# Reordering a chunk's last slot, the norm statistics and the first six front steps in a two-layer convolution kernel

## The chip, the cores and the metric

The kernel runs on one core of a Trainium2 chip. The metric is device time in microseconds: the median of several runs of the whole program, 5571.28 us for the kernel before (three runs, 5568.5 to 5586.93 us). One further execution was taken by the hardware profiler; every view below comes from it.

## The reference

Eight images of 256 channels and 64x64 pixels, float32, go through two layers with a residual each:

```
# layer 0, on gn(x): a group norm over 32 groups of channels
qkv = w_qkv . gn(x)                            # 1x1, 256 -> 768
attn = softmax(q . k over the 3x3 neighbours)  # 4 heads
out  = beta * (attn . v's 3x3 patches) + alpha * (generated 3x3 kernel . v's patches)
x1   = x + w_proj . out
# layer 1, on gn(x1): deformable 3x3 convolution
om   = conv3x3(gn(x1), w_off) + b_off          # 18 offsets and 9 masks for each pixel
v    = bilinear sample of gn(x1) at 9 shifted places, times sigmoid(mask)
y    = x1 + sum over the 9 places of w[:, :, place] . v
```

## The kernel before

**Two streams of work are woven into one order.** The *front* of an image is layer 0 and the preparation of layer 1: the generators `attention` (L550) and `prepare` (L617), run by `fronts` (L745), which stops at each `yield`. What lies between two yields is a *step*; an image has STEPS = 73 of them (L54). The *back* of an image is the sampling and the big convolution. Its unit is a *slot*: one of 9 places of one of 8 chunks of 8 rows (512 pixels), so 72 slots for an image. The loop at L875 walks over the 576 slots of all images and puts front steps between them. The order on TensorE (PE), ScalarE (ACT), VectorE (DVE) and GpSimd (POOL) is the order in which the Python code issues (`manual_schedule`, L854); the DMA queue of SyncE (SP) is ordered by the framework. PE's order, ACT's and DVE's are thus three lists made by the same walk, and a wait on one of them holds up whatever was issued behind it on that engine.

**The back.** Four *blocks* of 128 pixels make a slot. For each block `gather` (L758, POOL) fetches four corners of every pixel, 512 KB, by an indirect DMA into one of 10 buffers `g`; `scale` (L772, ACT) writes the first weighted corner to a buffer `s`; `sum_corners` (L783, DVE) adds the other three for two blocks at once, six instructions at line L788. `ahead(i)` (L792) issues two scales 8 blocks ahead of block i, the sums of two blocks 6 ahead, and two gathers 18 ahead (14 ahead in the last image, by LAST_GATHERS). `transposes` (L808) turns a slot's four `s` on PE (L815, tile `pt`) and copies them to `v` (L818, ACT, tile `vt`). `product` (L821) multiplies one slot's `v` with the weights of its place and accumulates in `po` (L832, PE), one PSUM tile with one buffer for a whole chunk. After a chunk's ninth product `finished` (L840) adds `po` and the residual in two DVE instructions (L843, tile `r`) and sends the result out from SP (L844). The next chunk's first product writes the same `po`, and so waits for L843.

**Order within slot n** (L875 to L891): transposes of slot n; `ahead(4n)`; product of slot n-1; the front steps that are due (one, and at times two); if slot n-1 ended a chunk, `finished`; `ahead(4n+2)`. I call a slot n with n divisible by 9 an *edge*. On DVE an edge therefore reads: sums 4n+6 and 4n+7, the step's DVE work, the two L843, sums 4n+8 and 4n+9.

**Steps.** A norm starts with `Norm` (L192): `bn_aggr` over a chunk-wise statistic (L199, DVE), a tiny matmul (L201, PE, tile `gn`) and four small DVE instructions; `ready` (L209) in the next step has a second tiny matmul (L212), a square root on ACT and a reciprocal; `normed` (L218, L228, DVE) then writes normalised rows `xn`. Each attention chunk has seven steps, which I name by their PE work:
A: `spread_weights` of the chunk before (L475 on PE, evacuated at L483 by DVE, tile `wk`, four PSUM buffers) and `q` (L276);
B: `k` (L308, evacuated by ACT);
C: `products` (L346, evacuated at L354 by DVE) and the first half of `weighted` (L516);
D: `logits` (DVE), the second half of the value transposes, `generated`;
E: first half of `v` (L308, evacuated at L330 by ACT), second half of `weighted`, `turned` (L398 on PE, L402 on DVE), `normed`;
F: second half of `v`, half of `project` (L528, added by DVE at L539), `softmax_3` (DVE);
G: the other half of `project`, statistics (L543), `weights` (L462), the first half of the value transposes.
Then come a closing step that projects the last chunk, the second norm, and nine preparation steps: `positions` (from L665; DVE from L682), `to_table` (L629), `offsets` (L649), statistics of the next image (L258). All these share four PSUM buffers, `ps_a` (L185), in turn: a PE group that needs a fifth waits until the first has been evacuated.

**Ahead of the loop** the whole front of image 0 and STEPS_AHEAD = 6 steps of image 1 (its first norm, then A to D of its first chunk) are issued (L859). After that 73 steps are spread over each 72 slots, so a period of 72 slots is the back of one image beside the front of the next; the last period has no front beside it.

Of the kernel before, what the change touches and what calls it, by code (L numbers as in the profile page):

```python
# [9 lines left out]
F32 = mybir.dt.float32  # L10
# [7 lines left out]
P = 128  # L18
C = 256
NT = C // P  # L20
# [5 lines left out]
NB = N // P  # L26
NC = H // R
KK = 9
# [18 lines left out]
SLOTS = NC * KK  # L47
BLOCKS = SLOTS * NB
SUM_AHEAD = 6
SCALE_AHEAD = SUM_AHEAD + 2  # L50
GATHERS = 10
LEAD = SCALE_AHEAD + GATHERS
LAST_GATHERS = 6
STEPS = 2 + 7 * NC + 6 + NC + 1  # L54
STEPS_AHEAD = 6

# [2 lines left out]
def preact_kernel(ctx: ExitStack, tc: tile.TileContext, a: dict, out: bass.AP):  # L59
# [19 lines left out]
    B = x.shape[0]  # L79
# [64 lines left out]
    with (  # L144
# [26 lines left out]
        for i in range(min(2, B)):  # L171
# [3 lines left out]
            for o in range(H * WP, ENTRIES, P):  # L175
                n = min(P, ENTRIES - o)
# [4 lines left out]
    p1 = ctx.enter_context(tc.tile_pool(name="p1", bufs=1))  # L181
# [7 lines left out]
    def psum_a(name):  # L189
        return ps_a.tile([P, 512], F32, tag="a", name=name)  # L190

    class Norm:  # L192


        def __init__(self, stats, name):
            self.name = name
            mv = p1.tile([P, NT, 2], F32, tag="mv", name=f"mv_{name}")
            for ct in range(NT):
                nc.vector.bn_aggr(mv[:, ct, :], stats[:, ct].rearrange("p c s -> p (c s)"))  # L199
            ps = psum_a(f"gn_{name}")  # L200
            nc.tensor.matmul(ps[:, 0:NT], gmat, mv[:, :, 0], start=True, stop=True)  # L201
            self.gn = gn = p2.tile([P, 2, NT], F32, tag="gn", name=f"gn_{name}")
            nc.vector.tensor_copy(gn[:, 0, :], ps[:, 0:NT])
            self.d = d = p1.tile([P, NT], F32, tag="gnd", name=f"gnd_{name}")
            nc.vector.tensor_sub(d, mv[:, :, 0], gn[:, 0, :])
            nc.vector.tensor_mul(d, d, d)
            nc.vector.tensor_add(d, d, mv[:, :, 1])
# [10 lines left out]
    def normed(xt, gn, c):  # L218

        xn = xn2[c % 2]  # L220
        lo, hi = max(0, R * c - 1), min(H, R * c + R + 1)
        if c == 0:
            nc.vector.memset(xn[:, :, 0, :], 0.0)
        if c == NC - 1:
            nc.vector.memset(xn[:, :, R + 1, :], 0.0)
        o = lo - (R * c - 1)
        for ct in range(NT):
            nc.vector.tensor_scalar(  # L228
                xn[:, ct, o : o + hi - lo, 1 : W + 1],
                xt[:, ct, lo * W : hi * W].rearrange("p (r w) -> p r w", w=W),  # L230
                gn[:, 0, ct : ct + 1],
                gn[:, 1, ct : ct + 1],
                ALU.subtract,
                ALU.mult,
            )
        return xn
# [13 lines left out]
        return t[:, ct, dy : dy + R, dx : dx + W]  # L250

    stats0: dict = {}

    def first_stats(b, c):
        if c == 0:
            stats0[b] = p2.tile([P, NT, NC, 6], F32, tag="stats0", name=f"stats0_{b}")
        for ct in range(NT):
            nc.vector.bn_stats(  # L258
                stats0[b][:, ct, c, :], image[:, ct, c * N : (c + 1) * N]
            )  # L260

    class Attention:

# [286 lines left out]
    def attention(b):  # L550

        xt = image
        gn = Norm(stats0.pop(b), f"0_{b}")
        stats = p2.tile([P, NT, NC, 6], F32, tag="stats", name=f"stats1_{b}")
        yield None
        gn = gn.ready()
        xn = normed(xt, gn, 0)
        yield None
        d = None
        for c in range(NC):  # L560
            a_ = Attention(b, c, xn, stats)
            if d:
                d.spread_weights()
            a_.q(0)
            a_.q(1)
            yield None
            a_.k(0)
            a_.k(1)
            yield None
            a_.products()  # L570
            if d:
                d.weighted(0)
            yield None
            a_.logits()
            if d:
                d.keys(1)
                d.carry_v()
            a_.generated()
            a_.softmax_1()
            a_.carry_k()  # L580
            yield None
            a_.v(0)
            if d:
                d.weighted(1)
            a_.turned()
            a_.softmax_2()
            if c + 1 < NC:
                xn = normed(xt, gn, c + 1)
            yield None
            a_.v(1)  # L590
            if d:
                d.add(0, d.project(0))
            a_.softmax_3()
            yield None
            if d:
                d.add(1, d.project(1))
                d.second_stats()
            a_.weights()
            a_.keys(0)
            yield None  # L600
            d = a_
        d.spread_weights()
        yield None
        d.weighted(0)
        d.keys(1)
        yield None
        d.weighted(1)
        yield None
        for m in range(NT):
            d.add(m, d.project(m))  # L610
        d.second_stats()
        yield None
        gn = Norm(stats, f"1_{b}")
        yield None
        yield gn.ready()

    def prepare(b, gn):  # L617
# [121 lines left out]
        if b + 1 < B:  # L739
            first_stats(b + 1, NC - 1)  # L740
# [17 lines left out]
    def gather(i):  # L758
        if i >= B * BLOCKS:
            return  # L760
        b, n = divmod(i, BLOCKS)
        c, k, j = n // NB // KK, n // NB % KK, n % NB
        g = gp.tile([P, 4 * C], F32, tag="g", name=f"g_{i}")
        nc.gpsimd.indirect_dma_start(  # L764
            out=g,
            out_offset=None,
            in_=tables[b % 2],
            in_offset=bass.IndirectOffsetOnAxis(ap=found[b, c][0][:, j, k : k + 1], axis=1),
        )
        rows[i] = g  # L770
# [21 lines left out]
    def ahead(i):  # L792

        scale(i + SCALE_AHEAD)
        scale(i + SCALE_AHEAD + 1)
        sum_corners(i + SUM_AHEAD)
        first = (B - 1) * BLOCKS
        for n in (i + LEAD, i + LEAD + 1):
            if n < first:
                gather(n)  # L800

        for n in (i + LEAD, i + LEAD + 1):
            if n - GATHERS + LAST_GATHERS >= first:
                gather(n - GATHERS + LAST_GATHERS)

    state: dict = {}

# [13 lines left out]
    def product(b, n):  # L821
        c, k = divmod(n, KK)
        if k == KK // 2:
            r = p1.tile([P, NT, N], F32, tag="r", name=f"r_{b}_{c}")
            nc.sync.dma_start(r, kept[b % 2][:, :, c * N : (c + 1) * N])
            state["r"] = r
        if k == 0:
            state["po"] = ps_o.tile([P, NT, 512], F32, tag="o", name=f"po_{b}_{c}")
        po, v = state["po"], state.pop(("v", n))
        for m in range(NT):  # L830
            for ct in range(NT):
                nc.tensor.matmul(  # L832
                    po[:, m, :],
                    w_conv[:, ct, k, m * P : (m + 1) * P],
                    v[:, ct, :],
                    start=(k == 0 and ct == 0),
                    stop=(k == KK - 1 and ct == NT - 1),
                )

    def finished(b, c):  # L840
        po, r = state["po"], state["r"]
        for m in range(NT):
            nc.vector.tensor_add(r[:, m], po[:, m], r[:, m])  # L843
        nc.sync.dma_start(  # L844
            out[b].rearrange("(t p) l -> p t l", p=P)[:, :, c * N : (c + 1) * N], r
        )
# [7 lines left out]
    with tc.manual_schedule(engines=ordered):  # L854
        for c in range(NC):
            first_stats(0, c)
        steps = fronts()
        done = 0
        while done < STEPS + STEPS_AHEAD:  # L859
            next(steps, None)  # L860
            done += 1
        for i in range(GATHERS):
            gather(i)
        for i in range(0, SUM_AHEAD, 2):
            if i == 0:
                scale(0)
                scale(1)
            scale(i + 2)
            scale(i + 3)
            sum_corners(i)  # L870
            gather(i + GATHERS)
            gather(i + GATHERS + 1)
        gather(SUM_AHEAD + GATHERS)
        gather(SUM_AHEAD + GATHERS + 1)
        for n in range(B * SLOTS + 1):  # L875
            if n < B * SLOTS:
                transposes(*divmod(n, SLOTS))
                ahead(NB * n)
            last = None
            if n > 0:  # L880
                b, h = divmod(n - 1, SLOTS)
                product(b, h)
                if h % KK == KK - 1:
                    last = b, h // KK
            while (done - STEPS - STEPS_AHEAD) * SLOTS < (n + 1) * STEPS:
                next(steps, None)
                done += 1
            if last:
                finished(*last)
            if n < B * SLOTS:  # L890
                ahead(NB * n + 2)  # L891


# [76 lines left out]
```

## Time and profile before

| what | value |
|---|---|
| median of three runs | 5571.28 us |
| the profiled execution: its own time | 5194.36 us |
| its span, first to last instruction | 5192.6 us |
| mean granted TensorE clock in it | 0.963 |
| from the start to the first product (L832) | 379.1 us |
| seven periods with a front beside them, each | 611 to 636 us |
| the last period, without one | 413.8 us |
| PE busy in the second period (628.2 us) | 586.0 us |
| DVE busy in it | 521.5 us |
| ACT busy in it | 293.1 us |

The profiled execution was 377 us (7%) shorter than the median of the runs, and nothing in the profile says why. Sums of durations below are made against 5194.36 us.

How to read the views: the page's first part gives busy time by engine (PEld is PE's weight load, which overlaps PE). The view by stretches gives busy time, granted clock (PEclk) and DMA load between two times. The view of waits says which engine stood idle before an instruction and what ended the idle time. The timeline lists instructions of an engine in order, equal neighbours merged: start, length, engine, line, operation, tiles out<-in, shape, count, and in brackets the idle time before them and who ended it.

### The profile page before, as it was taken

The page shows a single profiled execution, that of the slowest core. Times are in us where ns is not written, and L with a number is a line of the kernel's source. Part 1 is how long each engine was busy: PE and PEld are TensorE (multiplying, and loading weights), DVE is VectorE, ACT ScalarE, POOL GpSimd, SP SyncE. Part 2 cuts the span into 40 slices and gives each one's busy share as a digit, 9 for nine tenths or more (in the row PEclk, how much of TensorE's full clock was granted, in tenths as well). Part 3 has the DMA queues.
Part 4 walks back from the last instruction along what each step waited for, and adds up shares of the span by engine and source line. Part 5 has one row for each costly group of instructions (what it writes and reads, how often), then busy time and mean ns, then how long its engine had stood idle before and what let it go on. Part 6 is the DMA issues. An engine that isn't in the chain of part 4 may idle for free. (4 is left out here: it accounts for less than half of the span.)

```text
span 5192.6 us, 79716 instructions
## 1 busy us (share of the span) xinstructions
PE 4750.7 (91%) x26592; PEld 2643.4 (51%) x26592; DVE 4182.7 (81%) x10071; ACT 2360.6 (45%) x5184; POOL 3151.1 (61%) x2310
## 2 busy tenths in 40 slices
PE   6979999999999999989999999899999999998888
PEld 4545554555545555455554555445554455544443
DVE  4558788888888888788888888878888888877887
ACT  2334444444444444444444444444444444444544
POOL 0027665666657666566665666746666566666776
PEclk9989999999999999999999999999999999999999
DMA  2058778877797777977779777888778877788998
GB/s 91 21 180 277 266 273 304 300 267 257 275 322 280 268 269 260 337 262 273 279 267 324 273 260 262 287 291 285 268 265 296 297 274 267 267 296 313 388 379 337
DMA packets 476840, 1422.60 MB, mean 274 GB/s; under 512 B 46910, under 2 KB 114750, under 8 KB 476300
## 3 DMA queue, kind: packets, MB, share of 16 engines
q0 software_dynamic: 331776, 1208.11, 65.7%
q1 hardware_dynamic: 141902, 204.27, 11.0%
q10 hardware_dynamic: 2750, 5.12, 0.3%
q8 instruction: 210, 3.44, 0.3%
q14 instruction: 202, 1.65, 0.1%
HBM read 1280.19 MB, written 137.13 MB: 273 GB/s over the span
## 5 line engine op out<-in xcount | busy, mean ns | idle before, releaser
L764 POOL DMA_INDIRECT g<-table,idx x2304 | 3148.6, 1367 | 2019.3 <-DVE s L788 680.7
L788 DVE SCALAR_TENSOR_TENSOR s<-g,wt,s 128x256 f32<-128x256 f32 x6912 | 2798.4, 477 | 418.5 <-ACT s L780 407.4
L832 PE MATMUL po<-vt,w_conv 128*128 128x512 f32 x4608 | 2147.7, 610 | 95.9 <-DVE r L843 95.9
L832 PEld LDWEIGHTS po<-vt,w_conv 128*128 128x128 f32 x4608 | 858.3, 197 | 978.0 <-issue 870.6
L780 ACT ACTIVATE s<-g,wt 128x256 f32<-128x256 f32 x2304 | 1079.8, 509 | 480.6 <-DMA g<-table,idx 412.5
L815 PE MATMUL pt<-ident,s 128*128 128x128 f32 x4608 | 700.4, 285 | 104.1 <-DVE s L788 68.8
L815 PEld LDWEIGHTS pt<-ident,s 128*128 128x128 f32 x4608 | 520.9, 143 | 407.4 <-ACT vt L818 115.6
L818 ACT COPY vt<-pt 128x512 f32<-128x512 f32 x1152 | 610.7, 582 | 125.2 <-PE pt L815 124.7
L276 PE MATMUL psq<-xn,w_qkvT 128*128 128x512 f32 x512 | 301.3, 742 | 91.3 <-DVE wk L483 88.1
L284 ACT COPY q<-psq 128x512 f32<-128x512 f32 x128 | 75.0, 586 | 527.5 <-PE psq L276 527.5
L649 PE MATMUL om<-xn,w_off 128*32 128x512 f32 x2304 | 295.9, 611 | 8.6 <-DVE pos L682 8.6
L308 PE MATMUL psv<-xn,w_qkvT 128*128 128x264 f32 (+1 forms) x1088 | 260.6, 384 | 0.0
L354 DVE TENSOR_TENSOR qk<-qk,near_k 128x400 f32<-128x400 f32 x256 | 129.0, 565 | 161.1 <-PE qk L346 161.1
L276 PEld LDWEIGHTS psq<-xn,w_qkvT 128*128 128x128 f32 x512 | 115.8, 237 | 273.2 <-DVE wk L483 145.9
L308 PE MATMUL psk<-xn,w_qkvT 128*128 128x264 f32 (+1 forms) x1088 | 245.5, 380 | 0.0
L308 PEld LDWEIGHTS psv<-xn,w_qkvT 128*128 128x128 f32 x1088 | 201.7, 192 | 82.8 <-issue 50.1
L528 PE MATMUL proj<-acc,w_projT 128*128 128x512 f32 x512 | 238.2, 592 | 0.7 <-ACT acc L523 0.7
L308 PEld LDWEIGHTS psk<-xn,w_qkvT 128*128 128x128 f32 x1088 | 201.7, 190 | 59.8 <-issue 20.6
L330 ACT COPY v<-psv 128x320 f32<-128x320 f32 (+1 forms) x272 | 110.7, 418 | 249.5 <-PE psv L308 249.4
L321 ACT COPY k<-psk 128x264 f32<-128x264 f32 (+1 forms) x272 | 101.1, 372 | 214.7 <-PE psk L308 214.3
L523 ACT COPY acc<-av 128x512 f32<-128x512 f32 x128 | 74.9, 585 | 256.6 <-PE av L516 256.5
L483 DVE TENSOR_TENSOR wk<-wk,near 100x512 f32<-100x512 f32 x256 | 158.5, 680 | 32.3 <-PE wk L475 32.3
(89 smaller groups left out, 3296.8 us busy)
## 6 DMA issues: line engine op xcount, KB each, us to landing
table<-ts SPq DMA_DIRECT2D x384, 176.0 KB
g<-table,idx POOLq DMA_INDIRECT x2304, 6.3
x<-in_x_dram SPq DMA_DIRECT2D x64, 512.0 KB
x<-x SPq DMA_DIRECT2D x64, 512.0 KB
r<-x SPq DMA_DIRECT2D x64, 512.0 KB
out_dram<-r SPq DMA_DIRECT2D x64, 512.0 KB
w_conv<-in_w_conv_dram ACTq DMA_DIRECT2D x1, 2304.0 KB
w_qkv<-in_w_qkv_dram ACTq DMA_DIRECT2D x2, 384.0 KB
```

The lines of the kernel that those rows point to most:

```text
L276: nc.tensor.matmul(ps, w_qkvT[:, ct, m * P : (m + 1) * P], window(self.xn, ct, 4), start=(ct == 0), stop=(ct == NT - 1),)
L308: nc.tensor.matmul(ps[:, : (hi - lo) * WP], w_qkvT[:, ct, o : o + P], self.xn[:, ct, lo:hi, :], start=(ct == 0), stop=(ct == NT - 1),)
L354: nc.vector.tensor_mul(qk[:, 2 * jj : 2 * jj + 2, :, h, :], both[h][:, : 4 * NK].rearrange("p (j c k) -> p j c k", j=2, c=NT), near_k.unsq ...
L483: nc.vector.tensor_mul(wk.rearrange("p (t n) -> p t n", n=T * T), ps[:NK].rearrange("p (t n) -> p t n", n=T * T), near.unsqueeze(1).to_bro ...
L528: nc.tensor.matmul(ps, w_projT[:, ct, m * P : (m + 1) * P], self.acc[:, ct].rearrange("p (t y x) -> p y t x", y=T, x=T), start=(ct == 0), ...
L649: nc.tensor.matmul(ps[32 * g : 32 * g + 32, :], w_off[:, ct, k, :], window(xn, ct, k), start=(n < 4), stop=(n >= KK * NT - 4),)
L764: nc.gpsimd.indirect_dma_start(out=g, out_offset=None, in_=tables[b % 2], in_offset=bass.IndirectOffsetOnAxis(ap=found[b, c][0][:, j, k : ...
L780: nc.scalar.activation(s, g[:, 0:C], AF.Copy, scale=w[:, 0:1])
L788: nc.vector.scalar_tensor_tensor(s, g[:, q * C : (q + 1) * C], w[:, q : q + 1], s, ALU.mult, ALU.add)
L815: nc.tensor.transpose(pt[ct][:, j, :], s[:, ct * P : (ct + 1) * P], ident)
L818: nc.scalar.copy(v[:, ct, :], pt[ct].rearrange("p b n -> p (b n)"))
L832: nc.tensor.matmul(po[:, m, :], w_conv[:, ct, k, m * P : (m + 1) * P], v[:, ct, :], start=(k == 0 and ct == 0), stop=(k == KK - 1 and ct = ...
```

## The change

It has four parts.

1. At an edge `ahead(4n+2)` and `finished` are issued before the step. The order there becomes: transposes, `ahead(4n)`, `ahead(4n+2)`, product of slot n-1, `finished`, steps. At other slots the order stays.
2. `Norm` is cut in two. The `bn_aggr` instructions are issued in the step that makes the last of the statistics: for the first norm of an image at the end of the last `first_stats`, for the second at the end of the closing step. The rest, from the matmul L201 on, is the new method `means`, at the old place.
3. The six steps of image 1 are no longer issued ahead of the loop. The first period gets 79 steps in its 72 slots instead of 73; after it the count is the same as before.
4. LAST_GATHERS goes: `ahead` issues two gathers 18 blocks ahead in the last image too.

```diff
-LAST_GATHERS = 6
...
         def __init__(self, stats, name):
             self.name = name
-            mv = p1.tile([P, NT, 2], F32, tag="mv", name=f"mv_{name}")
+            self.mv = mv = p1.tile([P, NT, 2], F32, tag="mv", name=f"mv_{name}")
             for ct in range(NT):
                 nc.vector.bn_aggr(mv[:, ct, :], stats[:, ct].rearrange("p c s -> p (c s)"))
+
+        def means(self):
+            mv, name = self.mv, self.name
             ps = psum_a(f"gn_{name}")
...
     def first_stats(b, c):
...
+        if c == NC - 1:
+            norm0[b] = Norm(stats0[b], f"0_{b}")
...
-        gn = Norm(stats0.pop(b), f"0_{b}")
+        gn = norm0[b]
+        gn.means()
...
         d.second_stats()
+        gn = Norm(stats, f"1_{b}")
         yield None
-        gn = Norm(stats, f"1_{b}")
+        gn.means()
         yield None
         yield gn.ready()
...
         sum_corners(i + SUM_AHEAD)
-        first = (B - 1) * BLOCKS
-        for n in (i + LEAD, i + LEAD + 1):
-            if n < first:
-                gather(n)
-
-        for n in (i + LEAD, i + LEAD + 1):
-            if n - GATHERS + LAST_GATHERS >= first:
-                gather(n - GATHERS + LAST_GATHERS)
+        gather(i + LEAD)
+        gather(i + LEAD + 1)
...
-        while done < STEPS + STEPS_AHEAD:
+        while done < STEPS:
             next(steps, None)
             done += 1
...
         for n in range(B * SLOTS + 1):
+            last = None
+            if n > 0 and n % KK == 0:
+                last = divmod(n // KK - 1, NC)
             if n < B * SLOTS:
                 transposes(*divmod(n, SLOTS))
                 ahead(NB * n)
-            last = None
+                if last:
+                    ahead(NB * n + 2)
             if n > 0:
-                b, h = divmod(n - 1, SLOTS)
-                product(b, h)
-                if h % KK == KK - 1:
-                    last = b, h // KK
-            while (done - STEPS - STEPS_AHEAD) * SLOTS < (n + 1) * STEPS:
+                product(*divmod(n - 1, SLOTS))
+            if last:
+                finished(*last)
+
+            goal = (n + 1) * STEPS + min(n + 1, SLOTS) * STEPS_AHEAD
+            while (done - STEPS) * SLOTS < goal:
                 next(steps, None)
                 done += 1
-            if last:
-                finished(*last)
-            if n < B * SLOTS:
+            if n < B * SLOTS and not last:
                 ahead(NB * n + 2)
```

More of the change, by code (lines that the diff above doesn't have):

```diff
@@ L252, in preact_kernel @@
     stats0: dict = {}
+    norm0: dict = {}
     def first_stats(b, c):
```

## The prediction

> **What bounds the kernel now.** I read the page's first part, then the view by stretches, then PE's waits in one period, then timelines round the edges.
>
> ```profile
> PE 4750.7 (91%) x26592; PEld 2643.4 (51%) x26592; DVE 4182.7 (81%) x10071; ACT 2360.6 (45%) x5184; POOL 3151.1 (61%) x2310
> ...
> L832 PE MATMUL po<-vt,w_conv 128*128 128x512 f32 x4608 | 2147.7, 610 | 95.9 <-DVE r L843 95.9
> ...
> L780 ACT ACTIVATE s<-g,wt 128x256 f32<-128x256 f32 x2304 | 1079.8, 509 | 480.6 <-DMA g<-table,idx 412.5
> ```
>
> PE leads, and one place, L843, ends all idle time ahead of the products. By stretches, the second period, the last one, and a stretch after a stall:
>
> ```profile
> 1006.12:1634.32 628.20, 585.97 (x3321) 328.48 (x3321) 521.46 (x1259) 293.05 (x648) 406.68 (x288) 0.96 0.81 283
> 4773.74:5187.50 413.76, 363.16 (x1136) 169.95 (x1136) 352.22 (x855) 202.99 (x420) 313.33 (x273) 0.96 0.95 371
> 1233.40:1240.00 6.60, 6.60 (x10) 2.91 (x11) 4.69 (x12) 0.00 (x0) 3.63 (x2) 0.57 0.82 268
> ```
>
> Columns: length, busy PE, PEld, DVE, ACT, POOL, clock, DMA share. With a front beside it a period is PE's (586 of 628 us), with DVE close (521). The last period is rather the gathers' (DMA 0.95). PE's waits in the second period (total, times, longest):
>
> ```profile
> PE po L832 <- DVE r L843: 17.9, 7, 4.5
> PE psq L276 <- DVE wk L483: 12.6, 7, 2.2
> PE gn L201 <- DVE mv L199: 7.1, 2, 5.6
> ```
>
> So of 42 us idle per period the change aims at 25. Edge E of a chunk, in the timeline:
>
> ```profile
> 1223.03 3.60 PE L832 MATMUL po<-vt,w_conv 128*128 128x512 f32 x8
> ...
> 1233.40 6.53 PE L832 MATMUL po<-vt,w_conv 128*128 128x512 f32 x8 [2.53 <-DVE r L843]
> ...
> 1223.58 4.83 DVE L788 SCALAR_TENSOR_TENSOR s<-g,wt,s 128x256 f32<-128x256 f32 x12
> ...
> 1232.07 1.27 DVE L843 TENSOR_TENSOR r<-po,r 128x512 f32<-128x512 f32 x2
> ```
>
> The product behind the stall takes 6.53 us instead of 3.60: a stall costs its length and then a slower clock.
>
> [...] clock 0.57 for 6.6 us above; in the second period I count ten such windows of 3.4 or 6.8 us, 44 us at half clock in all, three behind L843 (13.7 us) and one behind L199 (6.8 us). [...] in the timeline L843 stands behind the step's DVE work though `po` was ready at 1226.6. [...]
>
> **Part 1, step behind the sums and L843.** No instruction is added. DVE's list becomes sums, sums, L843, step: before the step stand 2.45 us of sums (six at 0.41 us spacing) and 1.28 us of L843, so 3.73 us move from behind the step to ahead of it. PE gains where it waits for L843 and loses where it waits for the step. ACT gets two more scales ahead of the step's evacuations; each waits for its gather. On SP, L844's store comes ahead of the step's loads and stores; nothing shown waits for SP there. POOL's two gathers move ahead of nothing, as POOL has only gathers. By the edges of the second period:
>
> *Edge A (the step evacuates wk):*
>
> ```profile
> 1070.37 4.82 DVE L788 SCALAR_TENSOR_TENSOR s<-g,wt,s 128x256 f32<-128x256 f32 x12
> 1075.11 2.48 DVE L483 TENSOR_TENSOR wk<-wk,near 100x512 f32<-100x512 f32 x4
> 1077.50 1.28 DVE L843 TENSOR_TENSOR r<-po,r 128x512 f32<-128x512 f32 x2
> ...
> 1075.85 5.10 PE L276 MATMUL psq<-xn,w_qkvT 128*128 128x512 f32 x8 [2.21 <-DVE wk L483]
> ```
>
> Sums end at 1075.2; now +2.45 +1.28 = 1078.9 for L843 and +0.62 = 1079.55 for the first wk, which frees the buffer that psq waits for. It started at 1075.85: 3.75 us later, and idle for 6.0 us instead of 2.2, so about one more half-clock window: 1.25 us. Loss 5.0.
>
> *Edge E:* sums end 1228.4, +2.45 +1.28 = 1232.1, against 1233.34: 1.2 us gained, and with 1.3 us of idle left the half clock is not met: 6.53 - 3.60 = 2.9. Gain 4.1. Here DVE's step work after the sums was only some 3.7 us, as much as now comes ahead of it.
>
> *The others,* by the same sum: C: the second half of the av work waits for evacuations that come later, -1.35. G: L843 at 1314.05 instead of 1313.3, -0.75. B: 0. Closing step: +1.2, with the wait for its statistic. Preparation: L649 waits for a buffer that L682 frees, -1.5. Two steps at one edge (E+F): L843 ends at 1631.6 instead of 1634.26, +2.7, but ACT's two scales now stand ahead of the evacuations of `psv`:
>
> ```profile
> 1626.24 1.13 ACT L330 COPY v<-psv 128x160 f32<-128x160 f32 x4
> ...
> 1629.35 0.91 ACT L780 ACTIVATE s<-g,wt 128x256 f32<-128x256 f32 x2
> ```
>
> They wait for gathers that land at about 1629 and 1630.2 (issue 1622.7 plus 6.3 us median to landing), so the four evacuations slip to 1630.6 and `turned` by 4.3 us. What L843 gains is lost: 0.
>
> Sum: -5.0 -1.35 +4.1 -0.75 +0 +1.2 -1.5 +0 = -3.3 us per period.
>
> **Part 2, bn_aggr earlier.** It now runs ahead of 4.82 us of sums:
>
> ```profile
> 1576.40 4.82 DVE L788 SCALAR_TENSOR_TENSOR s<-g,wt,s 128x256 f32<-128x256 f32 x12
> 1581.14 0.60 DVE L199 BATCH_NORM_AGGREGATE mv<-stats 128x2 f32<-128x48 f32 x2
> ...
> 1581.79 0.59 PE L201 MATMUL gn<-mv,gmat 128*128 128x2 f32 x2 [5.58 <-DVE mv L199]
> ```
>
> The 5.58 us stall goes, but what is late next is the sums themselves: the transposes behind L201 need them, and they end 0.6 us later than before. PE's work from 1576 is then done sooner and waits at the transposes; I take 2.1 us (of the slot's half clock the most part), between 1.5 and 4.9. Parts 1 and 2: -3.3 + 2.1 = -1.2 us per period, 8.4 us over seven (range: plus or minus 6 a period, if half-clock windows fall otherwise).
>
> **Part 3, six steps into the first period.** Before:
>
> ```profile
> 365.01 3.29 ACT L780 ACTIVATE s<-g,wt 128x256 f32<-128x256 f32 x8
> ...
> 368.36 1.26 POOL L764 DMA_INDIRECT g<-table,idx  x1 [16.10 <-ACT s L780]
> ```
>
> The first scale stands behind the six steps (342.8 to 365.0 us: PE busy 15.1, DVE 8.7, ACT 5.8). The first gather went out at 340.0 and would be scaled from about 349. So the first product (379.12) comes about 17 us sooner, near 362. The steps' PE work, 12 to 13 us at full clock, goes to the first period, which PE fills. None of the six steps issues a DMA. Net gain 5, between 0 and 10: at worst all 17 comes back by stalls where two steps share a slot.
>
> **Part 4, LAST_GATHERS.** Nothing: POOL's list as built holds the same gathers in the same order with the same waits (each for the scale and sum of the block ten before, whose buffer it takes), as no other instruction lies between them on POOL. Cost 0 to 0.
>
> **Last period.** No steps there, so part 1 only puts 2.45 us of sums ahead of L843, at 7 edges. A slot takes 5.76 us, of which PE works about 5.0: 0.7 slack a slot, and the gathers lag some 2 us. I take 0.7 us an edge, 5 us; from 0 to 7 x 3.5 = 25.
>
> **Sum.** 8.4 - 5 + 5 = 8.4 us: 5194.4 becomes 5202.8, ratio 1.0016. The median of the runs is 1.0726 times the profiled execution; by the ratio 5571.3 becomes 5580.
>
> **Rivals.** *Waits change places* is the forecast: DVE's work is conserved, and whoever waited for L843 now waits for the step.
> *The stalls vanish (faster):* 17.9 + 7.1 us and their half clock (20.5 us at half speed, 10.2 lost) are 35 us a period, 247 in seven (-4.8%). For it: PE leads by 65 us, and DVE has 107 us of idle time a period to absorb shifts. Against: edges A and E as computed. I take a third, 80 us: 5485.
> *ACT held at edges (slower):* the two scales wait in ACT's queue for late gathers ahead of the evacuations. For it: 412.5 us of ACT's idle time end at a gather. It decides once the hold exceeds what four PSUM buffers cover, some 3.5 us of PE. At three edges a period, 4 us each and 1.7 of half clock: 17 us, 120 in seven (+2.3%). Half to full: centre 5636.
> *The change does nothing* is true of part 4, and of the sum within what can be told.
>
> **How the numbers follow.** About 0.3% (17 us) is what a measurement of this kernel can tell. Forecast 0.52, spread 5553 to 5620 by the bounds above: of it 0.02 faster, 0.28 same, 0.22 slower. Stalls vanish 0.30, faster. ACT held 0.18, slower. That is 0.32 faster, 0.28 same, 0.40 slower. The range, 5480 to 5640, takes in the forecast and the middle of both rivals; the forecast's own is 5553 to 5620.
>
> **What would show it.** In the profile after: the wait of L832 for L843 falls from 95.9 to some 50 us; that of L276 for L483 rises from 88.1 by 3.75 at each of seven A edges; L201's wait falls from 70.8 to below 30, and the transposes' wait for L788 (68.8) rises; the first product comes near 362 us; the first period is longer by about 12. The forecast is wrong if L832's wait goes and L276's doesn't grow (faster), or if PE's waits for L330, L284 or L818, all ACT, come to over 15 us a period (slower).

## The result, and the profile after

The changed kernel takes 5545.24 us (median of six runs, 5542.1 to 5555.23), the kernel before beside it 5589.03 us. The ratio on record, which is not the quotient of these two medians (that would be 0.9922), is 0.9938, with a 95% interval of 0.9918 to 0.9957: **0.6% faster**. The forecast was 5580 us, a ratio of 1.0016.

One thing has to be known ahead of any comparison. This kernel ran at two levels: about 5185 us or about 5550 to 5590 us, the same code at both. Each of the five chips whose numbers are on record was met once and showed one level throughout, so I speak of the level of a chip; that a chip keeps its level was not tested. The profiled execution of before, 5194.36 us, from which all stalls of the prediction were read, is of the first level; the runs that were compared, and the profile after, are of the second. The experiments' expectations call them the fast and the slow level; I write *5185 level* and *5550 level*. The kernels of one experiment's comparison ran on one chip.

The profile after, page (its lines are shifted: L833 is before's L832, L844 its L843, L787 its L780):

```profile
PE 4874.6 (88%) x26592; PEld 2725.8 (49%) x26592; DVE 4170.6 (75%) x10071; ACT 2368.6 (43%) x5184; POOL 3287.5 (59%) x2310
...
L833 PE MATMUL po<-vt,w_conv 128*128 128x512 f32 x4608 | 2187.8, 620 | 63.0 <-DVE r L844 37.4
...
L787 ACT ACTIVATE s<-g,wt 128x256 f32<-128x256 f32 x2304 | 1068.5, 509 | 562.5 <-DMA g<-table,idx 464.7
```

The second and the last period, by stretches (length, busy PE, PEld, DVE, ACT, POOL, clock, DMA share, GB/s):

```profile
1055.88:1713.30 657.42, 597.82 (x3320) 336.07 (x3321) 519.71 (x1259) 294.53 (x648) 414.42 (x289) 0.96 0.77 269
5000.59:5545.00 544.41, 391.42 (x1136) 195.33 (x1136) 349.00 (x850) 197.40 (x415) 384.34 (x273) 0.83 0.74 281
```

Against the second and the last period of the kernel before (628.2 us, and 418.9 us up to the end of the span; the stretch of 413.8 us shown ahead ends 5 us sooner) these are 29 and 125 us longer, in a kernel that is faster. So that profile can't be set beside this one; it needs a profile of the kernel before at the same level, which the first experiment gives. Its same two stretches:

```profile
1042.27:1714.86 672.59, 607.00 (x3320) 343.12 (x3320) 521.04 (x1259) 294.42 (x648) 410.93 (x288) 0.94 0.76 263
5008.36:5552.20 543.84, 390.34 (x1136) 192.86 (x1136) 353.11 (x856) 197.69 (x419) 360.06 (x275) 0.84 0.75 284
```

The long last period belongs to the level, not to the change. PE's waits over the whole span (total, times, longest), first the kernel before at this level, then the changed one:

```profile
PE pt L815 <- ACT vt L818: 139.3, 37, 10.3
PE po L832 <- DVE r L843: 131.5, 40, 8.7
PE qk L346 <- issue: 96.4, 179, 1.7
PE psq L276 <- DVE wk L483: 83.6, 43, 2.2
PE gn L201 <- DVE mv L199: 59.8, 9, 18.5
PE pt L815 <- DVE s L788: 34.3, 78, 6.5
```

```profile
PE pt L816 <- ACT vt L819: 129.9, 36, 9.7
PE psq L281 <- DVE wk L488: 108.4, 45, 5.8
PE pt L816 <- DVE s L795: 100.2, 108, 10.0
PE qk L351 <- issue: 75.4, 132, 1.7
PE gn L203 <- DVE mv L198: 40.3, 7, 19.0
PE po L833 <- DVE r L844: 37.4, 18, 3.3
```

Here too waits change places. Those for L843 and for L201's statistic fall by 94.1 and 19.5 us; those for wk and for the sums rise by 24.8 and 65.9 us. The four together go from 309 to 286 us (294 in the other profile of the changed kernel at this level). And the time at half clock (a granted clock of 0.5) in the six middle periods, added up from the trace's clock record, goes from 425 to 375 us (397 in the other profile), by estimate worth half of it: in the profile of the prediction the eleven products with 3.41 us of it take 5.40 us each, all that follow a stall without it 3.70. The result is a small balance of large terms. Where it is made is not settled: the middle six periods are 21 us shorter in this profile and 7 us in the other, the last one 1 us longer and 22 us shorter.

### The profile page after: what moved, and what is told of

Same layout as the page of the kernel before. It is cut to its first block, busy times and chain, and to the rows that moved or that the text cites. A ratio compares the mean times of both kernels' runs of the same rounds, so it can differ in the third digit from the quotient of the medians.

```text
span 5545.0 us, 79699 instructions
## 1 busy us (share of the span) xinstructions
PE 4874.6 (88%) x26592; PEld 2725.8 (49%) x26592; DVE 4170.6 (75%) x10071; ACT 2368.6 (43%) x5184; POOL 3287.5 (59%) x2310
## 5 line engine op out<-in xcount | busy, mean ns | idle before, releaser
L771 POOL DMA_INDIRECT g<-table,idx x2304 | 3284.9, 1426 | 2236.2 <-DVE s L795 585.5
L795 DVE SCALAR_TENSOR_TENSOR s<-g,wt,s 128x256 f32<-128x256 f32 x6912 | 2796.0, 478 | 566.5 <-ACT s L787 399.9
L833 PE MATMUL po<-vt,w_conv 128*128 128x512 f32 x4608 | 2187.8, 620 | 63.0 <-DVE r L844 37.4
L833 PEld LDWEIGHTS po<-vt,w_conv 128*128 128x128 f32 x4608 | 880.2, 202 | 965.9 <-issue 923.9
L787 ACT ACTIVATE s<-g,wt 128x256 f32<-128x256 f32 x2304 | 1068.5, 509 | 562.5 <-DMA g<-table,idx 464.7
L816 PE MATMUL pt<-ident,s 128*128 128x128 f32 x4608 | 725.0, 295 | 262.7 <-ACT vt L819 129.9
L816 PEld LDWEIGHTS pt<-ident,s 128*128 128x128 f32 x4608 | 547.4, 149 | 557.9 <-issue 184.4
L351 PE MATMUL qk<-k,q 64*64 64x100 f32 x4096 | 165.3, 260 | 78.5 <-issue 75.4
L351 PEld LDWEIGHTS qk<-k,q 64*64 64x64 f32 x4096 | 119.4, 136 | 155.0 <-issue 139.0
```

Of the source, the lines that this page charges most:

```text
L351: nc.tensor.matmul(both[h][64 * t : 64 * t + 64, n : n + NK], self.qt[r, ct, o * T * T : (o + 1) * T * T], kt[r, ct, :, T * o : T * o + KT ...
L771: nc.gpsimd.indirect_dma_start(out=g, out_offset=None, in_=tables[b % 2], in_offset=bass.IndirectOffsetOnAxis(ap=found[b, c][0][:, j, k : ...
L787: nc.scalar.activation(s, g[:, 0:C], AF.Copy, scale=w[:, 0:1])
L795: nc.vector.scalar_tensor_tensor(s, g[:, q * C : (q + 1) * C], w[:, q : q + 1], s, ALU.mult, ALU.add)
L816: nc.tensor.transpose(pt[ct][:, j, :], s[:, ct * P : (ct + 1) * P], ident)
L833: nc.tensor.matmul(po[:, m, :], w_conv[:, ct, k, m * P : (m + 1) * P], v[:, ct, :], start=(k == 0 and ct == 0), stop=(k == KK - 1 and ct = ...
```

## The experiments

"First product" is counted from the start of the span; "middle six" are periods 2 to 7 together; "last" runs from the last period's first product to the end of the span. Executions of one kernel on one chip scatter by some 10 us (standard deviation 7 to 12), and each row is one execution, or two. All profiled kernels at the 5185 level:

| kernel | first product | first period | middle six | last | ratio |
|---|---|---|---|---|---|
| before | 379.1 | 627.0 | 3767.6 | 418.9 | 1 |
| part 4 | 381.4 | 629.5 | 3763.4 | 420.7 | 1.0005 |
| L843 only | 379.7 | 618.6 | 3727.3 | 422.0 | 0.9909 |
| parts 1, 2 | 376.8 | 630.6 | 3768.3 | 407.7 | 1.0022 |
| 1, 2, 3, 4 | 359.6 | 661.1 | 3769.7 | 405.4 | 1.0029 |
| without 1 | 367.2 | 648.1 | 3767.5 | 417.5 | 1.0013 |
| without 2 | 363.2 | 663.0 | 3773.6 | 409.3 | 1.0060 |
| without 3 | 378.5 | 634.9 | 3766.6 | 407.3 | 1.0020 |
| without 4 | 362.9 | 659.8 | 3768.7 | 409.9 | 1.0029 |

and at the 5550 level, where the rows come from three chips and that of the first comparison, and the kernel before was profiled on one alone:

| kernel | first product | first period | middle six | last | ratio |
|---|---|---|---|---|---|
| before | 378.9 | 663.4 | 3966.1 | 543.8 | 0.998 |
| part 1 | 381.9, 377.4 | 673.0, 666.7 | 3990.4, 3949.1 | 543.3, 524.8 | 1.0041, 0.9979 |
| part 2 | 379.2 | 666.9 | 3982.5 | 553.9 | 0.9985 |
| part 3 | 363.1, 361.4 | 677.3, 683.8 | 3975.5, 3965.4 | 544.6, 545.1 | 1.0000, 1.0004 |
| 1, 2, 3, 4 | 367.0, 364.8 | 688.8, 680.2 | 3944.7, 3959.0 | 544.4, 522.3 | 0.9938, 0.9946 |
| without 1 | 364.9 | 686.7 | 3962.2 | 530.9 | 1.0000 |
| without 2 | 364.1 | 687.2 | 3987.2 | 530.7 | 1.0064 |
| L843 and part 2 | 384.4 | 652.9 | 3890.1 | 545.4 | 0.9867 |

**The kernel before again**, no edit.

> The kernel before, unchanged, to have a profile of an execution near the median. If the profiled execution of 5194 us was an exception, this one takes 5560 to 5600 us, the ratio is 1.000 within 0.3%, and its last period is about 535 us as in the changed kernel (not 414) and its periods with a front about 655 us (not 630). If the changed kernel itself brought the longer periods, they stay at 630 and 414 us here.

It met the 5550 level: profiled execution 5553.94 us, last period 544 us, middle six 3966 us. The longer periods are not the change's. Its ratio to itself was 0.998 (0.9965 to 0.9995). As the code is the same, a ratio at this level can be off by 0.2%, though its interval says less.

What is the level? DVE's waits in this profile have an entry that the profile of the 5185 level lacks:

```profile
DVE qk L354 <- remote: 160.4, 30, 7.9
DVE x L539 <- remote: 37.6, 7, 7.4
```

"remote" stands for a releaser that the profile can't name; ACT has 179.7 us of such waits at L818. They are zero in every profile at the 5185 level and over 200 us in each at the 5550 level. What DVE waits for is `qk` of PE, and PE's own list above shows 96.4 us of idle time ahead of L346 that end with "issue", which is also new: the records of its many small matmuls stand apart with nothing in the profile to wait for. In the last period it isn't seen on PE at all: at 5214.4 us ACT's L818, which needs the transposes, and DVE's L843, which needs the product, go on within 0.1 us of one another. PE's records of the transposes end at 5201.7, those of the product at 5205.2.

The trace's semaphore events, which the views do not print, say more. In the profile of the prediction 4634 instructions of PE name one semaphore to update, and the trace has 4634 updates of it. Here four of its updates land between 5214.33 and 5214.49 us, and none between 5198.7 and 5214.3. The transposes' and the product's thus come less than 0.2 us apart, though the product takes 3.6 us, and 9 us after its records end. I read this as work that was done, with its update late; the trace does not show which. Counted over a trace, 350 to 390 of PE's updates come more than 1 us (up to 13) after the last record that could have sent them in each profile at the 5550 level (351 in the profile after, the latest by 12.5 us), and 2 in each at the 5185 level. (At the 5550 level the traces lack 8 to 19% of the updates of PE, ACT and DVE, in the profile after 8.3, 16.5 and 13.5%, so this count is rough there, and so is the naming of who ended a wait. The idle time itself stands: ahead of all products 132.0 us here and 95.9 in the profile of the prediction.) Neither a lower full clock nor slower DMA packets explain it: a product ahead of which nothing stalled takes 3.60 us at both levels, and the median DMA packet of a gather 159 ns. What holds the updates back is not in the profile, and I leave it open.

**Part 1 alone.**

```diff
                 ahead(NB * n)
...
+                if last:
+                    ahead(NB * n + 2)
             if n > 0:
-                b, h = divmod(n - 1, SLOTS)
...
+                product(*divmod(n - 1, SLOTS))
+            if last:
+                finished(*last)
             while (done - STEPS - STEPS_AHEAD) * SLOTS < (n + 1) * STEPS:
...
-            if last:
-                finished(*last)
...
```

> Part 1 alone: at an edge the second sums and L843 ahead of the step. Waits-change-places (the forecast): +1.5 to +2.5 us a period and 0 to 25 in the last, so ratio 1.000 to 1.007. Edge theory (the 0.6% gain of the whole change is made here, as the products' wait for L843 falls from 96 to 37 us with nothing in its place): ratio 0.993 to 0.996. Start or gather theory: within 0.2% of 1.

1.0041 (1.0026 to 1.0056), within the forecast, and far from what the edge theory gave. The wait for L843 falls to 59.4 us, that for wk rises to 109.4 and that for the sums to 68.2.

**Part 2 alone.**

```diff
         d.second_stats()
+        gn = Norm(stats, f"1_{b}")
         yield None
-        gn = Norm(stats, f"1_{b}")
+        gn.means()
```

(and the same for the first norm, as in the change).

> Part 2 alone: the statistics are aggregated in the step that makes them. Forecast: 2.1 us a period (1.5 to 4.9), 15 us of 5590, ratio 0.994 to 0.998. If the transposes behind L201 take over the whole wait: 1.000. If it is the source of the whole gain: 0.994.

0.9985 (0.9972 to 0.9997). The wait of L201 falls from 59.8 to 31.3 us and that for the sums rises from 34.3 to 60.7: the transposes take it over, as the prediction feared. With the allowance above, a gain is not shown.

**Part 3 alone.**

```diff
-        while done < STEPS + STEPS_AHEAD:
+        while done < STEPS:
...
-            while (done - STEPS - STEPS_AHEAD) * SLOTS < (n + 1) * STEPS:
+            goal = (n + 1) * STEPS + min(n + 1, SLOTS) * STEPS_AHEAD
+            while (done - STEPS) * SLOTS < goal:
```

> Part 3 alone: six steps in the first period instead of ahead of the loop. Forecast: 5 us gained (0 to 10), ratio 0.998 to 1.000, with the first product 12 to 17 us sooner and the first period 10 to 15 us longer. Start theory (the first period has enough idle time to take the six steps for nothing): 17 us, ratio 0.997.

1.0000 (0.9985 to 1.0015), the top of the forecast: the first product comes 15.8 us sooner and the first period is 13.9 us longer.

**The changed kernel again.**

> The changed kernel again, beside the kernel before on the same chip in many executions. If its 0.6% is the code's, the ratio is 0.992 to 0.996 here too, and, as part 1 alone gave 1.004, part 2 0.9985 and part 3 1.000, the parts then work on one another. If the parts simply add up (1.004 x 0.9985 x 1.000 = 1.0025), the ratio is 1.000 to 1.005, and the 0.6% came with the few executions of the first comparison.

It met the 5185 level: 1.0029 (1.0018 to 1.0040). There the change is *slower*, 0.13% from the forecast of 1.0016 (how much of this is luck is said below). PE's waits in this profile, to be held against the prediction's last part:

```profile
PE psq L281 <- DVE wk L488: 111.6, 49, 5.8
PE pt L816 <- DVE s L795: 106.5, 155, 10.6
PE po L833 <- DVE r L844: 74.7, 36, 7.3
...
PE gn L203 <- DVE mv L198: 18.8, 2, 16.2
```

Edge A in the second period, whose rows before are in the prediction (PE, then DVE):

```profile
1094.15 6.67 PE L281 MATMUL psq<-xn,w_qkvT 128*128 128x512 f32 x8 [5.78 <-DVE wk L488]
...
1091.81 0.49 DVE L795 SCALAR_TENSOR_TENSOR s<-g,wt,s 128x256 f32<-128x256 f32 x1
1092.20 1.29 DVE L844 TENSOR_TENSOR r<-po,r 128x512 f32<-128x512 f32 x2
1093.40 2.49 DVE L488 TENSOR_TENSOR wk<-wk,near 100x512 f32<-100x512 f32 x4
```

The last of the sums (L795 here) and L843 (L844 here) now stand ahead of wk. The stall grew from 2.21 to 5.78 us and the matmuls behind it from 5.10 to 6.67 us: 5.1 us lost, where the prediction had 5.0.

**Parts 1 and 2.** The two edits above.

> Parts 1 and 2 without 3 and 4. If they add up: 1.0025, between 1.000 and 1.005. If the reordered edge needs the early statistics to pay (interaction): 0.993 to 0.997.

1.0022 (1.0012 to 1.0033), at the 5185 level: what adding up gave (1.0025), and not the 0.993 to 0.997 of an interaction.

**L843 alone ahead of the step.** Part 1 without its `ahead`:

```diff
             if n > 0:
-                b, h = divmod(n - 1, SLOTS)
...
+                product(*divmod(n - 1, SLOTS))
+            if last:
+                finished(*last)
             while (done - STEPS - STEPS_AHEAD) * SLOTS < (n + 1) * STEPS:
                 next(steps, None)
                 done += 1
-            if last:
-                finished(*last)
             if n < B * SLOTS:
                 ahead(NB * n + 2)
```

> Half of part 1: L843 ahead of the step, but the two sums 4n+8 and 4n+9 (with their scales and gathers) left behind it. If the 2.45 us of sums and the early scales are what made part 1 slower: L843 then comes before the step with only 1.28 us put ahead of it, the wait of the products for L843 falls from 130 to below 60 us and the wait for wk grows by less than 10 us, ratio 0.993 to 0.998. If it is L843 ahead of the step as such: 1.002 to 1.006 as for part 1.

**0.9909 (0.9891 to 0.9927)**, a larger gain than the 0.993 to 0.998 expected, with the middle six 40 us shorter than before's and 42 us shorter than the changed kernel's. PE's waits, and DVE at edge A in the second period:

```profile
PE psq L276 <- DVE wk L483: 107.9, 49, 3.4
PE pt L815 <- DVE s L788: 82.7, 147, 6.5
PE gn L201 <- DVE mv L199: 80.6, 16, 16.9
...
PE po L832 <- DVE r L843: 11.4, 15, 0.8
```

```profile
1071.04 1.29 DVE L843 TENSOR_TENSOR r<-po,r 128x512 f32<-128x512 f32 x2
1072.24 2.49 DVE L483 TENSOR_TENSOR wk<-wk,near 100x512 f32<-100x512 f32 x4
1074.63 2.47 DVE L788 SCALAR_TENSOR_TENSOR s<-g,wt,s 128x256 f32<-128x256 f32 x6
```

The 2.47 us of sums are behind wk again. The wait for L843 is gone (95.9 to 11.4 us), against 74.7 with the sums ahead. The wait for wk grew by 20 us, twice what I expected, but none is longer than 3.4 us, against 5.8. So part 1 loses what it wins with L843 by what it moves along. That is two scales, the sums and two gathers for each edge; that the sums cost the time is read from edge A, where they stand ahead of wk, and from PE's waits, while the three were not moved one by one.

**Part 4 alone.**

```diff
-        for n in (i + LEAD, i + LEAD + 1):
-            if n < first:
-                gather(n)
...
+        gather(i + LEAD)
+        gather(i + LEAD + 1)
```

> Part 4 alone: gathers 18 ahead in the last image too. Forecast: nothing, 1.000 within 0.2%, as the list of gathers and their waits is the same. Gather theory (gathers start sooner in the last period): 0.994 to 0.998, by a last period 10 to 30 us shorter than 535.

1.0005 (0.9994 to 1.0017), last period 420.7 against 418.9 us: nothing, as forecast.

**The changed kernel a third time.**

> The changed kernel a third time. The kernel before was seen at two levels, about 5190 us and about 5550 to 5590 us. If the sign of the change depends on the level (slower where the kernel runs in 5190 us, faster where it takes 5550 to 5590 us), the ratio is 1.003 at the first level and 0.994 at the second. If the first comparison was an exception, it is 1.000 to 1.005 at both.

It met the 5550 level: 0.9946 (0.9925 to 0.9966), as in the first comparison. The sign has gone with the level so far.

**Part 1 and part 3 once more.**

> Part 1 alone once more. It gave 1.0041 at the slow level. At the fast level, by the sum of stalls: 1.001 to 1.004, with the products' wait for L843 some 30 us smaller, the wait of psq for wk some 25 us and that of the transposes for the sums some 30 us larger, six middle periods together 0 to 20 us longer and the last period 10 us shorter. At the slow level 1.0041 again, within 0.2%.

> Part 3 alone once more. At the fast level, if it is what makes the first period of the changed kernel 34 us longer: first product 18 to 20 us sooner, first period 28 to 36 us longer, the others as before, ratio 1.002 to 1.003. If the longer first period needs parts 1 and 2: first period 10 to 15 us longer, ratio 0.998 to 1.000. At the slow level 1.000 again.

Both on the chip of the third time, at the 5550 level. Part 1: 0.9979 (0.9964 to 0.9995), a miss: not the 1.0041 of the other chip. The same edit thus differed by 0.6% from one chip to another, and a single ratio at this level is good to some 0.3 or 0.4%, whatever its interval. Part 3: 1.0004 (0.9992 to 1.0017), as before.

**L843 alone ahead, and part 2.** The edits of the two.

> L843 ahead of the step (the sums left behind it), and part 2, without parts 3 and 4. If they add up: 0.9909 x 0.9985 = 0.9894, between 0.987 and 0.992; the wait of L201 falls from 80 to below 40 us. If the transposes take over what L201 waited: 0.991. At the slow level L843 ahead of the step is untried: by the waits there (131 us of the products for L843) 0.98 to 0.99.

**0.9867 (0.9838 to 0.9895)** at the 5550 level, within the 0.98 to 0.99 expected: the fastest version there, and on the same chip 48 us below the changed kernel (5481.0 against 5528.6 us). The wait for L843 is 8.3 us, time at half clock in the middle six 321 us against 425. L201's wait is 47.2 us, not below 40. How much of the gain is part 2's was not run apart at this level.

**One part left out of the changed kernel.** Each is the changed kernel with the diff of one part, as above, taken back.

> The changed kernel without part 1 (edges in the old order). If the edges bring the gain at the slow level, as the products' wait for L843 is longer there (131 us against 96), it is lost: 0.998 to 1.000. If it comes from elsewhere: 0.993 to 0.996. At the fast level: 1.001 to 1.003, as part 3 alone costs 14 us there.

> The changed kernel without part 2 (statistics aggregated late). If part 2 is only its own 0.15%: 0.995 to 0.997 at the slow level. If parts 1 and 2 work together: 0.998 to 1.001. At the fast level: 1.003 to 1.006.

> The changed kernel without part 3 (six steps ahead of the loop again). If part 3 is neutral at the slow level: 0.993 to 0.996. At the fast level, without its 14 us: 0.999 to 1.002.

> The changed kernel without part 4 (gathers 14 ahead in the last image). Part 4 is nothing by the list of gathers: 0.993 to 0.996 at the slow level, 1.003 at the fast one. If it matters at the slow level, where the last period is longer: 0.998 to 1.000.

All four on one chip at the 5185 level: 1.0013 (0.9999 to 1.0027), 1.0060 (1.0038 to 1.0081), 1.0020 (1.0010 to 1.0030), 1.0029 (1.0019 to 1.0039). The kernel without part 4 agrees with all four parts on the other chip (1.0029), so the rest can be held against it on the same chip: without part 1 the median is 6.5 us lower, without part 2 12.4 us higher, without part 3 5.9 us lower. So part 2 gains some 0.24% beside the others; that parts 1 and 3 cost some 0.1% each is less than the 0.2% by which the kernel before differed from itself.

**The first two of them for the 5550 level.**

> The changed kernel without part 1, for the slow level. If the edges bring the gain there: 0.998 to 1.000. If part 2 brings it (its ratio alone was 0.9985 in one comparison): 0.993 to 0.996. At the fast level: 1.0013 again, within 0.15%.

> The changed kernel without part 2, for the slow level. If the edges alone bring the gain: 0.994 to 0.997. If the two parts are each needed: 0.998 to 1.001. At the fast level: 1.006 again, within 0.2%.

Without part 1: 1.0000 (0.9984 to 1.0015), within the range in which the edges bring the gain. Without part 2: 1.0064 (1.0040 to 1.0089), above both ranges expected: a miss. Each kernel with L843 or part 2 in its old form lies between 0.9979 and 1.0064, the two comparisons with both new at 0.9938 and 0.9946, and that with both but the sums in their old place at 0.9867. This fits a gain that needs both; it is not shown, as the changed kernel was not run on this chip, and part 1 alone differed by 0.6% between two.

## Why the prediction was wrong

**The step that failed is the last line of its sum:** "by the ratio 5571.3 becomes 5580". It read stalls from an execution of 5194 us and scaled their balance to runs of 5571 us, though nothing in the profile explained the difference between the two. At the level that was compared the waits are others: L843 ends 131.5 us of PE's idle time instead of 95.9 (longest 8.7 instead of 4.5 us), and half clock in the middle six is 425 us instead of 276. The middle six, which were to become 7 us longer, are 21 and 7 us shorter in the two profiles of the changed kernel there.

There was more to win ahead of L843: the changed kernel takes its wait to 37 and 53 us at the 5550 level, to 74.7 at the 5185 level, while wk's wait rises to 108 us (both profiles) and 112. That L843's larger wait turns the sign fits these profiles but is argued, not shown: part 1 alone, which takes that wait from 131.5 to 59.4 us in its first comparison, gave 1.0041 and 0.9979.

At the level it was read from, the total was near: forecast 1.0016, measured 1.0029 (1.0018 to 1.0040). **In good part that was luck.** Between the profiles of the two kernels at that level, one execution each, the start and the first period together are 14.6 us longer (forecast: 3.8 shorter), the middle six 2.1 us longer (forecast: 7.2), and the last period is 13.5 us shorter (forecast: 5 longer). The errors of the start and of the last period, some 18 us each, cancel.

Step by step, at the 5185 level:

- *Edge A, -5.0 us:* -5.1 in the second period. *wk's wait up by seven times 3.75 us, to 114:* 111.6. Right.
- *Edge E, 1.2 us gained on a stall of 2.53:* 1.16 us of stall are left. *Edge G, -0.75:* the stall went from 2.55 to 3.14 us. Right. *Edge E+F, 0:* its stall went from 4.46 to 0.84 us; what came back elsewhere is not separated.
- *L843's wait falls to some 50 us:* 74.7. Too hopeful. *The transposes' wait for the sums rises:* 68.8 to 106.5. Right, and the heart of it: the four waits (L843, L201's, wk, sums) go from 324 to 312 us, so most of the time changed places.
- *Parts 1 and 2 together, 7.2 us longer in six periods:* the middle six of the four kernels with both average 3768.3 us, of the two with neither 3765.5: 3 us. The same sign, and within the scatter of 10 us.
- *Part 2, 14.7 us in all:* with the other parts present, 12.4 us. Without part 1 it was run at the 5550 level only, and gave 0.9985 alone and 1.0000 with parts 3 and 4, not clear of the 0.2% allowed there. If the two depend on one another, the prediction did not have it.
- *Part 3, net gain 5:* wrong at this level, in size and, by the 5.9 us above, in sign. The first product came at 359.6 us (forecast 362), but the first period grew far more than by 12 us. By stretches, the changed kernel and the one without part 3:

```profile
359.56:1020.67 661.11, 604.60 (x3449) 340.26 (x3448) 529.32 (x1277) 301.45 (x669) 414.69 (x288) 0.96 0.76 267
```

```profile
378.50:1013.40 634.90, 583.68 (x3323) 327.45 (x3321) 520.33 (x1259) 297.06 (x652) 414.35 (x291) 0.97 0.79 280
```

  PE has 126 more matmul rows and 20.9 us more busy time, not 12 to 13; with 5.3 us more idle that makes 26 us for 19 won at the start. At the 5550 level the first period with part 3 alone was 14 and 20 us longer than the one profile of before there, for 16 and 18 us won.
- *Last period, +5:* it became some 12 us shorter with part 1 (405 to 410 us in five kernels, 417 to 422 in the four without). POOL is busy for less time there:

```profile
4790.39:5195.80 405.41, 357.33 (x1136) 171.88 (x1136) 350.82 (x850) 202.76 (x419) 294.93 (x272) 0.94 0.96 377
```

  294.9 us for 272 gathers, against 313.3 for 273 before. The difference lies in the long gathers, some 5 to 7 us each: 6 with 33 us in all instead of 8 with 51. With L843 alone ahead the last period stays at 422.0, so it is what else part 1 moves (scales, sums, gathers) that shortens it; that it does so by the long gathers is not shown, nor why these get fewer.
- *Part 4, nothing:* right.
- *Ten stretches of half clock in the second period, one more (1.25 us) at edge A, none left at edge E:* the last two were estimates. In the clock record of before (granted clock 0.5) seven of the ten last 3.41 us and three 6.83. Of the 3.41 us ahead of each, one had no record of PE, and in the other nine PE was busy for 0.9 to 2.0 us. At edge A the matmuls behind the stall took 1.57 us more (6.67 against 5.10). For edge E: the three products of before behind stalls of 1.41 to 1.60 us took 3.70 us each, as did nine of the profile after behind 1.15 to 1.53. But the length of a stall alone does not decide it: at edge E the stall was 2.53 us in each of the seven periods of before, and the product took 6.5 to 6.6 us in three and 3.70 in four.

Of the rivals, "the stalls vanish" had the sign at the 5550 level, not the mechanism: wk's wait and the sums' rose at both levels. It came nearer with L843 moved alone: the four waits go from 324 to 283 us at the 5185 level. "ACT held at edges" did not come: PE's waits for ACT's copies (L284, L330 and L818, by the lines of before) in the second period of the changed kernel are 3.7 us at the 5185 level and 3.1 at the 5550 level, against the 15 us that were named as its sign. Its centre, 5636 us, is a slip: that is half of its 120 us, and the middle between half and full is about 5668.

Open: what sets the level; why the sign goes with it; whether part 2 pays without part 1; why part 1 alone differs by 0.6% between two chips.

## What to carry to other kernels

Where a final sum waits behind other work in an engine's order, try to move that sum alone, and ask who waits for the work that it passes. Here 1.28 us moved ahead gained 0.9%, and the 2.45 us of other sums moved with it (and their scales and gathers) took the gain away at one level and more than half of it at the other. Look at a profile whose own time agrees with the median before scaling anything by a ratio: where the two differed by 7% here, the waits were others, and a balance of 0.2% had no sign. Try the parts of a change by leaving one out, as well as alone, and on the same chip.

## What the runs showed of the hardware

- The kernel before took 5166 to 5205 us on two chips and 5514 to 5572 us on three, and 5568 to 5599 us in the first comparison. At the second level ACT and DVE wait, up to 10 us at a time, with no releaser named (400.1 us in the kernel before, none at the first level), PE's small matmuls stand apart (96.4 us, none at the first level), and 350 to 390 of PE's semaphore updates come more than 1 us after the last record that could have sent them, against 2. The last period, which has no front, loses most (419 against 544 us).
- Some gathers take much longer to issue than the median of 0.94 us. In before at the 5185 level 115 of 2304 take over 3 us, up to 10, and they lie in all periods; in the last period 8 of 273, 6 to 7 us each. Before at the 5550 level has 120 of them, in its last period 11 of 275, 9 to 10 us each.
- A stall is often paid again by the matmuls behind it, at half clock (granted clock 0.50 from 1232.29 to 1239.12 us in before, at edge E). At edge A of the second period psq took 5.10 us after 2.21 us of stall, 5.14 after 3.41 (L843 moved alone) and 6.67 after 5.78; at edge E the product took 6.53 us after 2.53, against 3.60 without a stall. Not always: 2.29 us of stall left a product at 3.70 in all seven periods, and 2.53 us at edge E did so in four of them.
